# Moving four score steps in front of their slot's projections, and leaving out 18 idle transposes, in a one-core encoder-decoder kernel

## Chip, cores and metric

One Trainium2 chip, one core. The metric is the device time of one execution in microseconds, as the median of several runs. The traces are the hardware profiler's record of one further execution.

## The reference

An encoder layer over a short context, then a decoder layer over a long sequence, all in float32. D = 512, 16 heads of width 32, feed-forward width 2048, two batches, 2048 decoder tokens and 77 context tokens.

```python
x = src                                            # 2 x 77 x 512
x = x + mha(ln(x), ln(x), enc_weights, eb)
memory = x + ff(ln(x))
y = tgt                                            # 2 x 2048 x 512
y = y + mha(ln(y), ln(y), dec_sa_weights, sb)      # causal, with a relative bias
y = y + mha(ln(y), memory, dec_ca_weights, cb)     # cross attention, with a relative bias
y = y + ff(ln(y))
```

`mha` projects to queries, keys and values, takes `softmax(q k^T / sqrt(32) + bias)` per head, multiplies by the values and projects out.

## The kernel before

**Units.** The decoder's self attention is cut into units `(b, m, g, t)`: batch, block of 512 queries, group of four heads, tile of 128 queries; 128 units in all. For each unit the main loop at the end turns the probabilities on TensorE (`turn`, L425), copies them from PSUM (L429 on VectorE, L431 on ScalarE), runs the unit's *slot*, issues scores of a later unit (`scores`, L371), and multiplies by the values (`values`, L442). VectorE adds the bias to the scores and takes their maximum (L380, L387, then L397), and ScalarE takes the exponential (L402). In blocks with m = 0 the four exponentials of a unit are issued with its scores, so they stand in ScalarE's queue ahead of the copies of the turn that follows.

**Slots.** Everything else is hung on slots by hand. `slot(n)` issues three lists in order: `light[n]` (small steps: norms, divisions, loads), `jobs[n]` (projections: `q_job` L215, `k_job` L226, `v_job` L239, `out_job` L251), and `late[n]`. The order is written out: each engine runs its instructions in the order in which they are issued.

**What is in the slots.** The encoder is a chain of stages, put by `encoder()` into the first slots, nearly all into `late`. `score(1)` there (L563) is preceded by 18 transposes of the identity (L560), whose result nobody reads. The first block's cross attention is done inside the self attention of the second batch: `first_cross()` spreads it over slots 65 onwards. For each of four tiles of 128 tokens, t = 0 to 3, the steps are `score` (L783: 16 small products, each 32 rows by 77 columns, into four PSUM banks; then on VectorE for each of four heads L790 where there is a bias (t below 2), L792 and L793), `exp` (L796), `sums` (L801, L802), `normalize` (L807 on GpSimd), `turned` (L813), `times_v` (L824) and `out` (L833). `score` for tile t falls into slot 76 + 3t: slots 76, 79, 82 and 85. The projections in those slots are a key projection (L226), a query projection (L215), a value projection (L239) and a query projection (L215), each eight matmuls of 512 columns.

**Banks.** PSUM has eight banks; bank 7 is kept for the values and seven are given out in rotation, whoever asks:

```python
i = count["bank"] % count["banks"]
count["bank"] += 1
return psum[:, i, :]
```

A projection takes one bank, a score four, a piece of the unit's scores four, each load of a turn one. A step whose bank is still being read by VectorE or ScalarE waits on TensorE, and all that is issued behind it waits too.

## Time and profile before

| | |
|---|---|
| median of 3 runs | 2901.87 us (2894.16 to 2901.92) |
| the profiled execution | 2900.86 us, its span 2898.8 us |
| TensorE (PE) busy | 2861.1 us, 99% of the span |
| VectorE (DVE) busy | 2050.4 us, 71% |
| ScalarE (ACT) busy | 1298.8 us, 45% |
| mean granted TensorE clock | 0.992 |
| slots 76, 79, 82, 85 | score's products start at 1016.9, 1043.5, 1085.1 and 1126.2 us |
| encoder's second score | idle transposes start at 95.2 us, score's products at 97.3 us |

In lines of the trace the first two numbers are the start and the duration in microseconds, then engine, source line, operation, what is written from what, the shapes, and a count; in brackets stands how long the engine idled before it and which instruction ended that. PEld is the loading of weights on TensorE, which runs ahead of the matmuls. A matmul's end is modelled, so small waits hide in it; the distance from one start to the next is the safer measure. A line that covers several instructions merges neighbours of one kind.

### The profile page before, as it was taken

Reading aid. Unit: us, or ns where it says so; the run is one execution under the profiler, and the core shown is the slowest. Engines: PE = TensorE matmul, PEld = TensorE weight load, DVE = VectorE, ACT = ScalarE, POOL = GpSimd, SP = SyncE. Lnnn points to the kernel's source line nnn. Section 1 sums busy time; section 2 is a strip of 40 time slices with the busy share of each in tenths; the row PEclk is TensorE's granted clock in tenths of the full one; section 3 lists DMA queues with packets and bytes.
Section 4 is the critical chain, followed back from the end, with each engine's and each line's share of the span. In section 5 each row is a group of like instructions: output and inputs, shape, how many; then the busy total and the mean of one; then the engine's idle time right before and its main releaser. Section 6 shows DMA issues by size and latency. Waiting matters only on the chain.

```text
span 2898.8 us, 60382 instructions
## 1 busy us (share of the span) xinstructions
PE 2861.1 (99%) x24456; PEld 2025.4 (70%) x24456; DVE 2050.4 (71%) x5566; ACT 1298.8 (45%) x2431; POOL 745.5 (26%) x605
## 2 busy tenths in 40 slices
PE   9899999999999999999999999999999999999999
PEld 5557666666666556666666677777777777777788
DVE  4767688878986668788878895757575757575745
ACT  3344465546665445565556674323232323232321
POOL 0100000000000101100000004464646464646464
PEclk9899999999999999999999999999999999999999
DMA  6413301201112502201201115100002000000000
GB/s 171 116 32 122 107 16 56 63 16 45 34 42 64 138 19 61 76 27 56 63 16 38 42 31 173 37 30 1 29 1 47 1 30 1 30 1 30 1 15 15
DMA packets 118456, 137.34 MB, mean 47 GB/s; under 512 B 18544, under 2 KB 73888, under 8 KB 118050
## 3 DMA queue, kind: packets, MB, share of 16 engines
q1 hardware_dynamic: 118178, 133.49, 15.9%
q8 instruction: 192, 3.15, 0.5%
q14 instruction: 86, 0.70, 0.1%
HBM read 111.59 MB, written 21.86 MB: 46 GB/s over the span
## 4 chain that ended last, share of the span: by engine, by line
PE 93%; DVE 4%; ACT 1%; DMA 1%; issue 1%; SPq 0%; POOL 0%; DVEq 0%; ACTq 0%; POOLq 0%
PE psum L425 17%; PE psum L1198 14%; PE psum L1169 13%; PE psum L371 11%; PE psum L442 9%; PE psum L833 4%; PE psum L768 4%; PE psum L239 4%; PE psum L251 4%; PE psum L215 3%; PE psum L226 3%; PE psum L813 2%; PE psum L783 1%; PE psum L824 1%; ACT pp L402 1%; PE psum L543 1%
## 5 line engine op out<-in xcount | busy, mean ns | idle before, releaser
L402 ACT ACTIVATE pp<-pp,nm 128x128 f32<-128x128 f32 (+15 forms) x512 | 611.6, 1200 | 274.8 <-DVE nm L397 274.6
L380 DVE TENSOR_SCALAR_CACHE_REDUCE pp<-psum 128x512 f32<-128x512 f32 (+3 forms) x1024 | 559.2, 590 | 58.2 <-PE psum L371 56.7
L425 PEld LDWEIGHTS psum<-ident,pp 128*128 128x128 f32 x4352 | 477.2, 143 | 114.6 <-DVE pp L380 51.9
L425 PE MATMUL psum<-ident,pp 128*128 128x128 f32 x4352 | 541.6, 279 | 11.0 <-DVE mx L387 4.4
L431 ACT COPY pts<-psum 128x512 f32<-128x512 f32 (+3 forms) x592 | 297.8, 574 | 477.0 <-PE psum L425 370.9
L1152 POOL TENSOR_TENSOR vv<-pp 128x512 f32<-128x512 f32 x320 | 418.3, 1323 | 153.3 <-PE psum L1169 132.0
L429 DVE COPY pts<-psum 128x512 f32<-128x512 f32 (+2 forms) x544 | 330.0, 659 | 69.0 <-PE psum L425 68.7
L371 PE MATMUL psum<-kT,q 32*128 32x512 f32 (+3 forms) x2560 | 369.0, 577 | 9.8 <-ACT pts L431 4.8
L442 PEld LDWEIGHTS psum<-pts,vv 128*32 128x32 f32 x8704 | 227.3, 110 | 125.4 <-issue 117.3
L442 PE MATMUL psum<-pts,vv 128*32 128x128 f32 x8704 | 280.9, 277 | 0.7 <-ACT pts L431 0.5
L285 POOL TENSOR_TENSOR rstd<-rstd,mhalf 128x1 f32<-128x1 f32 x32 | 18.2, 570 | 881.4 <-DVE rstd L284 881.4
L1184 DVE TENSOR_TENSOR kT<-kT,psum 128x512 f32<-128x512 f32 x256 | 166.0, 680 | 111.5 <-PE psum L1169 102.9
L371 PEld LDWEIGHTS psum<-kT,q 32*128 32x128 f32 x2560 | 128.2, 184 | 148.1 <-issue 86.4
L387 DVE CUSTOM_DVE_ANT_0 pp<-psum,bias 128x256 f32<-128x256 f32 (+1 forms) x512 | 195.9, 411 | 16.4 <-PE psum L371 16.4
L1187 ACT ACTIVATE kT<-kT,vecs 128x256 f32<-128x256 f32 x256 | 115.2, 499 | 176.1 <-DVE kT L1184 176.1
L1198 PE MATMUL psum<-vv 128*128 128x256 f32 x768 | 176.9, 381 | 0.0
L1169 PE MATMUL psum<-oT,vv 128*128 128x256 f32 x736 | 166.5, 380 | 0.0
L1198 PEld LDWEIGHTS psum<-vv 128*128 128x128 f32 x768 | 143.1, 190 | 26.8 <-issue 9.5
L1182 ACT COPY kT<-psum 128x512 f32<-128x512 f32 x124 | 69.6, 588 | 205.3 <-DVE kT L1184 134.9
L1169 PEld LDWEIGHTS psum<-oT,vv 128*128 128x128 f32 x736 | 138.8, 190 | 24.4 <-issue 6.2
L1152 DVE TENSOR_TENSOR vv<-kT 128x512 f32<-128x512 f32 x160 | 136.3, 866 | 12.4 <-PE psum L1198 11.5
L266 POOL TENSOR_TENSOR xr<-xr,row_dec_sa_out_b 128x512 f32<-128x512 f32 x30 | 38.2, 1275 | 370.1 <-DMA xr<-in_x_dram 367.4
(182 smaller groups left out, 3881.1 us busy)
## 6 DMA issues: line engine op xcount, KB each, us to landing
wqk<-in_dec_sa_in_wT_dram SPq DMA_DIRECT2D x64, 256.0 KB, 3.7
bias<-tzg SPq DMA_DIRECT2D x128, 128.0 KB, 3.8
wbig<-in_dec_sa_in_wT_dram SPq DMA_DIRECT2D x8, 1024.0 KB, 5.2
vv<-in_enc_ff_wT_dram SPq DMA_DIRECT2D x8, 1024.0 KB, 5.4
wbig<-in_dec_sa_out_wT_dram SPq DMA_DIRECT2D x8, 1024.0 KB, 5.8
vv<-y SPq DMA_DIRECT2D x32, 256.0 KB, 3.8
out_dram<-vv SPq DMA_DIRECT2D x32, 256.0 KB, 2.0
xt<-in_x_dram SPq DMA_DIRECT2D x30, 256.0 KB, 3.1
```

Of the source, the lines that this page charges most:

```text
L371: nc.tensor.matmul(banks[r][:, : kn * P], q[rows4(r), ts(t, P)], kT[rows4(r), g, k0 * P : (k0 + kn) * P], start=True, stop=True,)
L380: nc.vector.tensor_scalar(p[:, k0 * P : (k0 + far) * P], s[:, : far * P], 1.0, None, ALU.mult, ALU.max, accum_out=st["mx"][:, r, c : c + 1],)
L387: nc.vector.tensor_tensor_reduce(p[:, (i + 1) * P - w : (i + 1) * P], s[:, far * P : kn * P], biases[b, m, g][:, r, 2 * P - w :], 1.0, LOW ...
L402: nc.scalar.activation(p, p, AF.Exp, bias=nm, accum_out=to)
L425: nc.tensor.transpose(pt[:, ts(x, P)], state[n]["p"][r][:, ts(k, P)], ident)
L429: nc.vector.tensor_copy(pts[:, : len(load), :], pt[:, :w])
L431: nc.scalar.copy(pts[:, : len(load), :], pt[:, :w])
L442: nc.tensor.matmul(ot[rows4(r), t, :], vv[:, k, ts(g * HC + r, HD)], got.pop((n, k, r)), start=(k == 0), stop=(k == i),)
L1152: engine.tensor_tensor(dst, quarter(*parts[0], n), quarter(*parts[2], n), SIGN[parts[1]])
L1169: nc.tensor.matmul(mm[:, ts(f, TOK)], a[:, c, ts(f, P)], b[:, c, :], start=(c == 0), stop=(c == 1))
L1184: nc.vector.tensor_tensor(dst, dst, got, SIGN[sign])
L1198: nc.tensor.matmul(mm[:, t, :], lhs[:, c, ts(t, P)], rhs[:, c, :], start=(n == 0 and c == 0), stop=(n == 3 and c == 1),)
```

## The change

The four `score` steps of `first_cross` go from `late` (behind the slot's projection) into `light` (ahead of it). They are entered last into their lists, so they stand behind the slot's other small steps: the division, and `out` of an earlier tile (slots 82 and 85) and the third norm (slot 85). The other steps keep their lists and order. In the encoder the 18 transposes at `score(1)` are gone. No instruction is added; the number of banks taken in each slot is unchanged, their order within the slot isn't.

```diff
             def score(b):
                 banks = [bank() for _ in range(HC)]
-                if b:
-                    for _ in range(18):
-                        nc.tensor.transpose(banks[0][:, :P], ident, ident)
                 for g in range(NC):
...
-            plan, behind = {}, {}
-
-            def at(slot, f, plan=plan):
+            plan = {}
+
+            def at(slot, f):
                 plan.setdefault(slot, []).append(f)
...
                 for k, f in zip((0, 1, 2, 2, 4, 5, 6), fs):
-                    at(11 + 3 * t + k, f, plan if k else behind)
+                    at(11 + 3 * t + k, f)
...
-            return plan, behind
+            return plan
...
-        for fs_of, to in zip(first_cross(), (light, late)):
-            for r, fs in fs_of.items():
-                to[len(units) // 2 + 1 + r] += fs
+        for r, fs in first_cross().items():
+            light[len(units) // 2 + 1 + r] += fs
```

## The prediction

> **What bounds the kernel now.** I read the page first: busy shares and the chain that ended last.

> ```profile
> PE 2861.1 (99%) x24456; PEld 2025.4 (70%) x24456; DVE 2050.4 (71%) x5566; ACT 1298.8 (45%) x2431; POOL 745.5 (26%) x605
> ...
> PE 93%; DVE 4%; ACT 1%; DMA 1%; issue 1%; SPq 0%; POOL 0%; DVEq 0%; ACTq 0%; POOLq 0%
> ```

> TensorE is the bound, so the change is worth what it does to TensorE's stops and to its clock. The table of 4 us windows around the first two scores shows both; the columns are PE, PEld, DVE, ACT, POOL busy (count), granted clock, DMA.

> ```profile
> 1020.00:1024.00 4.00, 1.31 (x15) 0.46 (x3) 3.83 (x9) 0.00 (x0) 0.00 (x0) 0.75 0.00 0
> 1024.00:1028.00 4.00, 3.85 (x9) 2.14 (x10) 1.69 (x12) 2.58 (x10) 0.00 (x0) 0.50 0.00 0
> 1028.00:1032.00 4.00, 4.00 (x23) 1.50 (x22) 1.80 (x5) 1.41 (x3) 0.00 (x0) 0.90 0.00 0
> ...
> 1048.00:1052.00 4.00, 2.64 (x6) 1.28 (x6) 3.86 (x11) 0.00 (x0) 0.00 (x0) 0.66 0.00 0
> 1052.00:1056.00 4.00, 4.00 (x19) 3.59 (x18) 2.88 (x14) 1.27 (x3) 0.00 (x0) 0.50 0.00 0
> ```

> After the scores of slots 76 and 79 PE stops, DVE is full, and the clock is at half. From the means: 0.75 over 4 us is 2 us at half, so it fell at 1022.0; 0.90 in the third row ends it at 1028.8. The second stretch runs likewise from 1049.3 to 1056.1. Then I read the timeline in order of time. Slot 76:

> ```profile
> 1013.33 3.60 PE L226 MATMUL psum<-nT,wqk 128*128 128x512 f32 x8
> ...
> 1016.86 1.13 PE L783 MATMUL psum<-pp 32*128 32x77 f32 x32
> ...
> 1018.01 0.48 DVE L790 TENSOR_TENSOR pp<-psum,pp 128x308 f32<-128x308 f32 x1 [3.16 <-PE psum L783]
> ...
> 1021.37 0.33 PE L425 MATMUL psum<-ident,pp 128*128 128x128 f32 x1 [0.86 <-DVE pp L790]
> ...
> 1024.15 0.48 PE L425 MATMUL psum<-ident,pp 128*128 128x128 f32 x1 [0.89 <-DVE mx L387]
> ...
> 1025.40 5.30 PE L239 MATMUL psum<-wbig,nT 128*128 128x512 f32 x8
> ```

> DVE idles 3.16 us while the key projection runs; then the score's twelve DVE operations (L790, L792, L793 for four heads) hold the banks and keep L387 back, and PE waits. Slot 79:

> ```profile
> 1043.53 0.83 ACT L431 COPY pts<-psum 128x384 f32<-128x384 f32 x2
> ...
> 1044.04 0.86 PEld L783 LDWEIGHTS psum<-pp 32*128 32x128 f32 x26 [0.28 <-ACT pts L431]
> ...
> 1049.77 1.22 PE L371 MATMUL psum<-kT,q 32*128 32x256 f32 x2 [0.72 <-DVE pp L790]
> ```

> Score already waits for ACT there, and PE later waits for DVE. Slot 82:

> ```profile
> 1085.18 0.69 DVE L242 TENSOR_TENSOR vv<-psum,row_sa_bv 128x512 f32<-128x512 f32 x1 [2.74 <-PE psum L239]
> ...
> 1086.30 0.48 DVE L792 TENSOR_REDUCE cmx<-psum 128x4 f32<-128x308 f32 x1 [0.43 <-PE psum L783]
> ...
> 1095.31 0.42 PEld L425 LDWEIGHTS psum<-ident,pp 128*128 128x128 f32 x4 [0.27 <-DVE mx L387]
> ```

> Slot 82 again has a DVE that idles during the projection (2.74 us) and is late afterwards. Last, the encoder's idle turns:

> ```profile
> 95.20 2.19 PE L560 MATMUL psum<-ident 128*128 128x128 f32 x18
> ...
> 98.90 0.83 ACT L431 COPY pts<-psum 128x384 f32<-128x384 f32 x2
> ...
> 99.41 0.71 PE L563 MATMUL psum<-pp 32*77 32x77 f32 x26 [1.73 <-ACT pts L431]
> ```

> **The change part by part.** Score's 16 products (32 instructions) stay as many; PE's work moves by 0.9 us (L783's start 1016.86 to the next weights at 1017.75) and the projection's 3.53 us changes place with it. Score issues no DMA, and POOL and SP are passed by nothing. One SP issue moves with slot 79's projection: the weights that reuse its buffer (L199, 1043.56) go out some 5 us later; slot 83's query projection needs them only at 1097.

> *Which bank.* The turn ahead of slot 76 or 79 fills four of seven banks. Before, the projection took the first free bank, score the next four, so its third head took the turn's first bank, which ACT empties. Now score starts one bank earlier, and its fourth head takes that bank. The projection stands behind that wait in PE's queue.

> *Slot 76.* Score issues at 1013.2, three heads go, the fourth waits for ACT: the copies start at 1013.84 and the first gives its bank 0.51 later (1043.53 to 1044.04 in slot 79), so at 1014.35. From there 0.96 us to the first L790 (1044.04 to 1045.00): 1015.3 instead of 1018.01. The chain to the first L387 took 5.66 us (1018.01 to 1023.67): 1020.97, and PE's fourth turn follows 0.48 later at 1021.45, not 1024.15. PE's own path: projection 1015.2 to 1018.75, scores 0.65, values 1.01, three turns to 1020.6; a wait of 0.9 us is left. L461 and the third L387 put L239's weights at 1022.2 instead of 1025.19. At full clock L239 takes 3.63 us (the next one, 1032.83 to 1036.46), here it took 5.44. So PE is through at 1025.85 instead of 1030.63: **-4.8**. I take the clock to stay, since a key projection and L239 now stand within 4 us of the gap; if it falls all the same, the gain is the 3.0 us of earlier start alone.

> *Slot 79.* Here the same wait is long: score issues at 1039.8, and ACT has four exponentials ahead (1040.70 to 1043.53), so PE stands from 1040.2 to 1044.04, 3.8 us in which the query projection used to run. Score's DVE work starts at 1045.00, as before. The projection runs 1044.9 to 1048.5 beside it; its eviction L217 (0.75 us) now queues behind score's twelve on DVE, and the unit's L380 behind that: 1050.65 + 0.75 = 1051.4, four L380 of 0.48 to 1053.3, L387 0.42, so the next turn's last bank comes at 1053.75. A turn of 0.45 and L813's 1.9 end at 1056.1 against L226's start at 1057.65: -1.5 at best. But 3.8 us of standing should drop the clock. A half-clock stretch of 3.4 to 6.8 us costs PE 1.7 to 3.4; PE's own path from 1048.5 through scores, values, scores, turns and L813 (0.9 + 0.9 + 0.8 + 1.85 + 1.95) ends at 1054.9, so 1056.6 to 1058.3, or 1059.1 if score itself is slowed. Bounds -1.5 and +1.4; I take **-0.5**, by the shorter stretch.

> *Slots 82 and 85.* The copies are done long before (1075.90 to 1079.95, against a score at 1081.5), so no new wait. Slot 82: score's DVE work starts at 1081.5 + 1.22 = 82.7 and takes 3.68 (1086.30 to 1089.98), to 1086.4; L242 0.65, and the first L380 starts at 1087.05 instead of 1089.98, 2.9 earlier, while PE comes to the same L371 at 1086.0. From there PE's work by undisturbed rows is 1.07 + 1.44 + 1.07 + 28 turns x 0.108 = 6.6 us, to 1092.6, the last bank comes at 1092.3; L813 starts at 1092.8 instead of 1095.70: **-2.9**. Slot 85 by the same sum: **-2.8** (DVE 1131.05 to 1128.2). The low end is what PE's rows call idle in 1085.0 to 1097.4 and 1126.2 to 1137.6: 0.4 and 0.24 each.

> Does a gain last? From 1097 to 1126 PE's starts follow each other without a gap, and the later transfers hang on the same steps, so I let it stand.

> *Idle turns.* 18 transposes, 2.19 us of PE, gone; but what follows waits for ACT's copy at 98.90 to 99.35, which nothing on PE moves. Gain zero: PE stands from 95.5 to 99.4 instead. The cost is the clock, which falls anyway at 100.4 and returns at 107.2 (0.55 and 0.60 in the windows from 100 and 104). If it falls 3.4 us sooner, L563 and the work up to 100.4 run slower: 0 to 1.7 us; I take **+0.6**, about L563's 0.7 us doubled.

> *Sum.* -4.8 - 0.5 - 2.9 - 2.8 + 0.6 = -10.4 against the profiled execution's 2900.86 (span 2898.8 and 2.1 around it): 2890.5. That execution lies 1.0 under the median, so 2891 to 2891.5; I say 2891.

> [...] The clock row at 1048 to 1052 fell with PE listed busy 2.64 of 4 us and no idle over 0.72 us; the work was narrow (32-row scores). [...]

> **The rivals.** *The gain is mostly given back* (2896): the clock still falls in slot 76 (-3.0), slot 79 takes +1.4, and slots 82 and 85 save half (-2.8), since DVE is full after 1128 too (3.90 of 4 us) and another release comes late; with +0.6 that is -3.8, or 2897; spread 2894 to 2902. For it: DVE's fullness. Against it: DVE itself starts 2.7 to 2.9 us earlier in three slots.

> *ACT's copy is late in all four slots* (slower): if the exponentials stood ahead of the copies in 82 and 85 as in 79, PE would stand some 3.8 us in each, with a clock stretch each time: 4 x 1.4 + 1.7 = +7.3, 2908; spread 2903 to 2916. It decides once the bank comes about 4 us after score's issue, since then DVE starts no earlier than before. For it: the row at 1044.04. Against it: in slot 76 the bank is 1.1 us away, and in 82 and 85 free.

> That the change does not do what it says I leave at nothing: all four go ahead of a projection.

> **How the numbers follow.** A measurement here can tell about 0.3%, 8.7 us, from no change. Forecast (2884 to 2894): 0.52. Given back: 0.36. Slower: 0.12. The border for faster is 2893.2, which leaves 0.50 faster; the rest of the forecast, the second case and the part of the third under 2910.6 make 0.43 the same; 0.07 slower. The forecast's own range is 2884 to 2894. The range of 2885 to 2901 leaves out the slow case and the tips of the others, under 2 in 10.

> **What would show it.** Right: L783 ahead of L226, L215, L239, L215; slot 76 with a short wait for L431, L239 in about 3.7 us and the clock at 1; slot 79 with a wait of near 3.8 us for L431 and one half-clock stretch over the projection; L380 about 2.9 us sooner after the scores of 82 and 85. Wrong: waits for L431 in 82 or 85, a clock that stays at half beyond 6.8 us in slot 79 or longer in the encoder, or PE gaps of 2 to 3 us that turn up between the slots.

## The result and the profile after

The kernel after takes 2891.58 us (median of 11 runs, 2889.82 to 2894.04) against 2899.01 for the kernel before (11 runs, 2894.16 to 2901.92): a ratio of 0.9974, 95% interval 0.9965 to 0.9983, so 7.4 us less. Repeated in the last set of experiments, it was 2890.91 against 2899.08, ratio 0.9971 (0.996 to 0.9983). The forecast was 2891, in a range of 2885 to 2901; as a difference, -10.4 was forecast and -7.4 measured. The profiled execution took 2889.82 us, the lowest of the 11. In the kernel after the score's lines are three lower: L780 for L783, L787, L789 and L790 for L790, L792 and L793, L810 for L813, L560 for L563.

The page first: TensorE's busy time and the shares of the chain of waits.

```profile
PE 2852.6 (99%) x24438; PEld 2021.1 (70%) x24438; DVE 2048.3 (71%) x5566; ACT 1299.5 (45%) x2431; POOL 746.3 (26%) x605
...
PE 93%; DVE 4%; ACT 1%; DMA 1%; issue 1%; SPq 0%; POOL 0%; DVEq 0%; ACTq 0%; POOLq 0%
```

Nothing there tells where 7 us went; the bound is the same. The windows of 4 us at slots 76 (two rows) and 79 (three) tell it; the columns are those of the tables of before, with the granted clock third from the end.

```profile
1016.00:1020.00 4.00, 3.78 (x51) 2.26 (x50) 3.86 (x15) 0.69 (x1) 0.00 (x0) 1.00 0.25 70
1020.00:1024.00 4.00, 4.00 (x16) 1.45 (x14) 1.68 (x4) 3.94 (x12) 0.00 (x0) 1.00 0.00 0
...
1032.00:1036.00 4.00, 1.44 (x12) 0.98 (x10) 2.08 (x9) 2.78 (x8) 0.00 (x0) 0.97 0.46 124
1036.00:1040.00 4.00, 3.43 (x28) 2.62 (x29) 1.75 (x4) 0.89 (x4) 0.00 (x0) 0.50 0.06 14
1040.00:1044.00 4.00, 4.00 (x7) 1.39 (x5) 3.72 (x9) 0.00 (x0) 0.00 (x0) 0.68 0.00 0
```

In slot 76 PE hardly stops and the clock stays at 1. In slot 79 PE stands (busy 1.44 of 4 us) and the clock is at half from 1035.7 to 1042.6. The timeline of slot 76:

```profile
1011.72 1.11 PE L780 MATMUL psum<-pp 32*128 32x77 f32 x26 [0.58 <-ACT pts L431]
...
1012.66 0.48 DVE L787 TENSOR_TENSOR pp<-psum,pp 128x308 f32<-128x308 f32 x1 [0.56 <-PE psum L780]
...
1018.80 0.33 PE L425 MATMUL psum<-ident,pp 128*128 128x128 f32 x1 [0.21 <-DVE mx L387]
...
1019.63 3.60 PE L239 MATMUL psum<-wbig,nT 128*128 128x512 f32 x8
```

The fourth head waits shortly for ACT's copy, VectorE begins beside the key projection, the waits of 0.86, 1.08 and 0.89 us ahead of the turns are down to one of 0.21, and L239 takes 3.60 instead of 5.30 us. Slot 79:

```profile
1036.57 1.99 PE L780 MATMUL psum<-pp 32*128 32x77 f32 x26 [3.08 <-ACT pts L431]
1038.48 5.70 PE L215 MATMUL psum<-nT,wqk 128*128 128x512 f32 x8
```

Here is the long wait for the copy, and the projection behind it, at half clock for most of its 5.70 us. Slot 82: VectorE's score work, the projection's eviction, the first L380, and the turns' end.

```profile
1075.08 0.48 DVE L789 TENSOR_REDUCE cmx<-psum 128x4 f32<-128x308 f32 x1 [0.42 <-PE psum L780]
...
1078.76 0.68 DVE L242 TENSOR_TENSOR vv<-psum,row_sa_bv 128x512 f32<-128x512 f32 x1
1079.71 0.69 DVE L380 TENSOR_SCALAR_CACHE_REDUCE pp<-psum 128x512 f32<-128x512 f32 x1 [0.27 <-PE psum L371]
...
1085.62 1.91 PE L810 MATMUL psum<-ident,pp 128*77 128x128 f32 x16
```

L242 follows the score's work without an idle time; the 2.74 us of idling are gone.

**Lining up two traces.** Every unit has one L397 on VectorE. Its start in one run minus its start in the kernel before, unit by unit, is a running balance. In the kernel after it stands at -2.74 us ahead of slot 76, and then steps: -4.73 over slot 76, -0.32 over slot 79, -2.40 over slot 82, -2.41 over slot 85, together **-9.86**. It then stays at -12.6 for 370 us, and at 1500 us steps back by +2.1, to -10.44, where it stays. Nothing that the change touches is there. The same work in the timelines, before and then after:

```profile
1509.53 5.14 PE L371 MATMUL psum<-kT,q 32*128 32x256 f32 x18 [0.33 <-DVE pp L380]
1514.60 2.66 PE L425 MATMUL psum<-ident,pp 128*128 128x128 f32 x20
```

```profile
1496.97 6.09 PE L371 MATMUL psum<-kT,q 32*128 32x256 f32 x18 [0.33 <-DVE pp L380]
1503.00 4.22 PE L425 MATMUL psum<-ident,pp 128*128 128x128 f32 x20
```

and the windows there, two of before and then three of after:

```profile
1508.00:1512.00 4.00, 3.67 (x23) 1.95 (x16) 3.68 (x15) 0.00 (x0) 0.00 (x0) 1.00 0.00 0
1512.00:1516.00 4.00, 4.00 (x25) 2.47 (x21) 3.96 (x16) 0.66 (x2) 0.00 (x0) 1.00 0.00 0
```

```profile
1496.00:1500.00 4.00, 3.67 (x22) 2.15 (x18) 3.78 (x15) 0.00 (x0) 0.00 (x0) 0.99 0.00 0
1500.00:1504.00 4.00, 4.00 (x14) 2.18 (x12) 3.97 (x16) 0.00 (x0) 0.00 (x0) 0.50 0.00 0
1504.00:1508.00 4.00, 4.00 (x23) 3.76 (x22) 2.44 (x7) 3.27 (x4) 0.00 (x0) 0.65 0.00 0
```

A half-clock stretch of 6.9 us (0.08 + 4 + 2.8) that the profile of before does not have. The -2.74 ahead of slot 76 is mostly the reverse: the stretch that the profile of before has at 646 us is missing in this one, 2.3 us, and 0.8 us is from the start of the program.

### The profile page after: what moved, and what is told of

It is laid out like the page before. It is cut to its first block, busy times and chain, and to the rows that moved or that the text cites. A ratio compares the mean times of both kernels' runs of the same rounds, so it can differ in the third digit from the quotient of the medians.

```text
span 2888.0 us, 60347 instructions
## 1 busy us (share of the span) xinstructions
PE 2852.6 (99%) x24438; PEld 2021.1 (70%) x24438; DVE 2048.3 (71%) x5566; ACT 1299.5 (45%) x2431; POOL 746.3 (26%) x605
## 4 chain that ended last, share of the span: by engine, by line
PE 93%; DVE 4%; ACT 1%; DMA 1%; issue 1%; SPq 0%; POOL 0%; DVEq 0%; ACTq 0%; POOLq 0%
PE psum L425 17%; PE psum L1194 14%; PE psum L1165 13%; PE psum L371 11%; PE psum L442 8%; PE psum L830 4%; PE psum L765 4%; PE psum L239 4%; PE psum L251 4%; PE psum L215 4%; PE psum L226 3%; PE psum L810 2%; PE psum L780 1%; ACT pp L402 1%; PE psum L821 1%; PE psum L543 1%
## 5 line engine op out<-in xcount | busy, mean ns | idle before, releaser
L380 DVE TENSOR_SCALAR_CACHE_REDUCE pp<-psum 128x512 f32<-128x512 f32 (+3 forms) x1024 | 559.1, 590 | 58.1 <-PE psum L371 56.6
L425 PEld LDWEIGHTS psum<-ident,pp 128*128 128x128 f32 x4352 | 475.0, 142 | 110.2 <-DVE pp L380 51.6
L425 PE MATMUL psum<-ident,pp 128*128 128x128 f32 x4352 | 537.6, 278 | 8.3 <-DVE mx L387 3.7
L431 ACT COPY pts<-psum 128x512 f32<-128x512 f32 (+3 forms) x592 | 297.9, 575 | 473.2 <-PE psum L425 367.0
L371 PE MATMUL psum<-kT,q 32*128 32x512 f32 (+3 forms) x2560 | 362.4, 578 | 5.8 <-ACT pts L431 3.0
L371 PEld LDWEIGHTS psum<-kT,q 32*128 32x128 f32 x2560 | 125.6, 184 | 143.2 <-issue 88.6
L387 DVE CUSTOM_DVE_ANT_0 pp<-psum,bias 128x256 f32<-128x256 f32 (+1 forms) x512 | 195.8, 410 | 16.4 <-PE psum L371 16.4
L1148 DVE TENSOR_TENSOR vv<-kT 128x512 f32<-128x512 f32 x160 | 135.2, 859 | 13.4 <-PE psum L1194 12.4
```

The costliest lines, as they stand in the source:

```text
L371: nc.tensor.matmul(banks[r][:, : kn * P], q[rows4(r), ts(t, P)], kT[rows4(r), g, k0 * P : (k0 + kn) * P], start=True, stop=True,)
L380: nc.vector.tensor_scalar(p[:, k0 * P : (k0 + far) * P], s[:, : far * P], 1.0, None, ALU.mult, ALU.max, accum_out=st["mx"][:, r, c : c + 1],)
L387: nc.vector.tensor_tensor_reduce(p[:, (i + 1) * P - w : (i + 1) * P], s[:, far * P : kn * P], biases[b, m, g][:, r, 2 * P - w :], 1.0, LOW ...
L425: nc.tensor.transpose(pt[:, ts(x, P)], state[n]["p"][r][:, ts(k, P)], ident)
L431: nc.scalar.copy(pts[:, : len(load), :], pt[:, :w])
L1148: engine.tensor_tensor(dst, quarter(*parts[0], n), quarter(*parts[2], n), SIGN[parts[1]])
```

## The experiments

Theory after the result: the four slots give 9.9 us of the 11.0 forecast, and about 2 us go back to half-clock stretches later, which the shift of the work brings about. Rival: some slot gives less in most runs than in this one profile, or the missing turns in the encoder cost it.

**The idle turns alone.**

```diff
-                if b:
-                    for _ in range(18):
-                        nc.tensor.transpose(banks[0][:, :P], ident, ident)
```

> Only the 18 idle turns are left out of the kernel before; the scores stay behind their projections. Theory (the turns filled a wait for ScalarE's copy and only put off the fall of the clock): between 0 and +1.7 us, +0.6 likeliest; in the trace the wait for L431 ahead of L563's 26 weights grows from 1.7 to some 3 us, and the clock falls at about 97 us instead of 100.4. Rival A (the turns were on the path): -2.2 us. Rival B (without them the clock stays low): +3 us or more.

2899.6 against 2899.0 us, ratio 1.0003 (0.9994 to 1.0011). The balance steps by +0.42 between the units around 95 us. Of the trace, PE's wait and the windows:

```profile
99.47 1.19 PE L560 MATMUL psum<-pp 32*77 32x77 f32 x26 [3.16 <-ACT pts L431]
...
96.00:100.00 4.00, 0.84 (x18) 0.69 (x22) 3.69 (x11) 3.88 (x11) 2.49 (x3) 0.67 0.70 126
```

The wait for the copy grew from 1.73 to 3.16 us and the clock fell at 97.4 instead of 100.4; the copy came when it came. The turns were off the path, and by the balance rivals A and B fall; the whole time alone (-1.7 to +3.2 us by its interval) would leave room for B.

**The scores alone.** The turns are put back into the kernel after.

> Only the four scores are moved; the 18 idle turns stay. Theory (all of the gain is in the four slots): the traces of before and after give -4.75, -0.5, -2.4 and -2.4 in slots 76, 79, 82 and 85, so -10 us if nothing is given back. Rival (part is given back between the slots or by the clock elsewhere): -7 us or less, with the missing part to be found in the trace behind slot 85. The turns alone can't explain the difference if they cost under 1 us.

2892.11 against 2899.0, ratio 0.9977 (0.9967 to 0.9986): -6.9. The slots give -4.73, -0.12, -2.40 and -2.41, so -9.66, and at 1502 us the balance steps back by 2.2. The rival: part is given back, and not by the turns.

**One slot at a time.** In the kernel before, the condition that sends a score into the later list is narrowed to some tiles: `t in (0,)`, `t in (1,)`, `t in (2, 3)`.

```diff
-                    at(11 + 3 * t + k, f, plan if k else behind)
+                    at(11 + 3 * t + k, f, plan if k or t in (0,) else behind)
```

> Only tile 0's score (slot 76) is moved; turns stay. Theory (earlier start of the score's VectorE work, 3.0 us, and a clock that no longer falls, 1.8 us): -4.8 us, with the granted clock at 1 through slot 76 and L239 in about 3.7 us. Rival (start alone, clock still falls): -3.0 us. The half-clock stretch of slot 79 stays in either case.

> Only tile 1's score (slot 79) is moved; turns stay. Theory (a stop of some 3.5 us for L431 and a half-clock stretch over the projection, against the VectorE wait and the half-clock stretch that go): -0.5 us, between -1.5 and +1.4. Rival (the stop is what counts): +3 us or more.

> Only the scores of tiles 2 and 3 (slots 82 and 85) are moved; turns stay. Theory (VectorE's idle stretch during the projection takes the score's work): -4.8 us, 2.4 in each slot, and no wait for L431 at the score. Rival (VectorE is full soon after and gives it back): -2 us or less.

| moved | measured against before | ratio, interval | slots, by the balance | later steps of the balance |
|---|---|---|---|---|
| slot 76 | -0.5 us | 0.9998 (0.9989 to 1.0007) | 76: -4.73, 79: +0.58 | +1.6 at 1382, +2.1 at 1508 us |
| slot 79 | +2.1 | 1.0008 (0.9999 to 1.0017) | 79: -0.70 | +1.6 at 1385, +2.1 at 1512 |
| slots 82, 85 | -4.6 | 0.9985 (0.9976 to 0.9994) | -2.40, -2.41 | +1.6 at 1383 |

Each slot does by itself what it does in the whole, within 0.4 us; moving slot 76 alone also shifts the unchanged slot 79 by +0.58. But the medians of the parts, -0.5 + 2.1 - 4.6 and +0.6 for the turns, make -2.4 and not -7.4; on the whole time the expectation for slot 76 was missed by 4 us and that for slot 79 by 2.6, while that for slots 82 and 85 was met within 0.2. The difference stands in the last column: two stretches of narrow work far behind the slots, at about 1383 and 1512 us of the kernel before, which have the full clock there, run at half clock in these kernels. In the run with slot 76 alone, the windows at slot 76 and at the two places:

```profile
1018.00:1022.00 4.00, 3.77 (x51) 2.33 (x44) 3.52 (x15) 1.12 (x4) 0.00 (x0) 1.00 0.24 66
...
1384.00:1388.00 4.00, 4.00 (x62) 3.67 (x54) 1.70 (x5) 2.22 (x5) 1.79 (x2) 0.80 0.16 38
1508.00:1512.00 4.00, 4.00 (x14) 2.08 (x12) 3.96 (x18) 0.00 (x0) 0.00 (x0) 0.56 0.00 0
```

So slot 76 itself behaves as foretold (clock at 1, -4.73), and the whole hides it.

**Shifting the work on purpose.** Idle transposes behind the four slots move all later work without changing it: 22 or 11 in the kernel after, 10 in the kernel before. They write into the bank that is due next, so the rotation of the banks stays.

```diff
+        def stand(k):
+            for _ in range(k):
+                nc.tensor.transpose(psum[:, count["bank"] % count["banks"], :P], ident, ident)
+
+        light[100].append(lambda: stand(10))
```

> The kernel before, with 10 idle transposes (1.07 us) in slot 100. Theory of the grid: the narrow scores at about 1512 us, which keep the full clock in the kernel before, come onto the bad place, so it costs +3.2 us against the kernel before, with a half-clock stretch at about 1513 us in the trace. Rival: +1.1 us and no new stretch.

2902.48 against 2899.08, ratio 1.0011 (1.0002 to 1.002): +3.4. The balance steps by +1.10 at the transposes and by +2.05 at 1511 us, where the clock is now at half:

```profile
1508.00:1512.00 4.00, 3.67 (x17) 2.49 (x16) 3.97 (x18) 0.00 (x0) 0.00 (x0) 0.90 0.00 0
1512.00:1516.00 4.00, 4.00 (x16) 2.18 (x12) 4.00 (x15) 0.38 (x1) 0.00 (x0) 0.50 0.00 0
```

As expected: 1.1 us of delay cost 3.4. The kernel before owes full clock in that place to where the work happens to lie.

> The kernel after, with 22 idle transposes (22 x 0.107 = 2.4 us of TensorE) put into slot 100, behind the four slots. Theory (the half-clock stretches come on a grid of 3.41 us whose place to the work is nearly the same in every run; the change's gain moved the narrow scores near the end of the last block but one onto a bad place of the grid, which takes 2.1 us back at about 1500 us): 2.4 us later the scores lie as in the kernel before, the stretch at 1500 us is gone, and the kernel costs 0 to +0.5 us against the kernel after. Rival (the stretches fall at random, or are none of the gain's doing): +2.4 us.

2894.25 us, 3.3 over the kernel after measured beside it (2890.91, below). The stretch at 1500 us is gone, as expected, but one of two lengths came up at 1378, which I had reckoned safe: the balance steps by +2.40 at the transposes, by +3.24 at 1378, and by nothing at 1500. Half of the expectation held, the total did not.

> The same with 11 idle transposes (1.2 us). Theory of the grid: the narrow work at about 1375 us comes onto the bad place too (1.6 us, as in the runs that moved one slot alone), so it costs between +0.7 and +2.8 us against the kernel after, that is as much as twice 1.2 us or as much as the 22 transposes. Rival: +1.2 us.

2888.14 us, 2.8 **under** the kernel after. In its profile the stretch at 1500 is gone and one of 3.4 us stands at 1374 (+1.6); with the transposes' 1.2 that makes +0.7 behind the four slots, as expected. The profiled execution (2887.57) also lacks the stretches at 520 and 646 us, 3.9 us in all by the balance against the kernel before. They lie ahead of the transposes, which can't have removed them; so it is not shown that the useless work made the kernel faster. Its seven runs lie in two groups, four near 2888 and three from 2891 to 2893, and only the first group's 2887.57 has a profile. On the whole time the expected sign was wrong, and I could not say in advance which narrow place falls.

> The kernel after once more, on the same chip as the three runs with idle transposes: 7.4 us under the kernel before as in its first runs, with a half-clock stretch at about 1500 us and one in slot 79.

2890.91 us, ratio 0.9971 (0.996 to 0.9983); stretches at 1038 (slot 79) and 1502 us, the slots -4.73, -0.18, -2.40 and -2.41.

**What still stands in slot 79.** Two ways against the wait for ACT's copy, both in the kernel after. One only fills it:

```diff
+                        if fill and g == 0 and r == 3:
+                            for _ in range(fill):
+                                nc.tensor.transpose(banks[0][:, 3 * P :], ident, ident)
```

> The kernel after, with 30 idle transposes of the identity in slot 79 between the third head and the fourth of the score, where TensorE stands for L431; they add nothing to the path as long as the wait is over 3.2 us. Theory (the half clock in slot 79 comes of the stop): the clock stays at 1 there, L215 takes 3.6 instead of 5.7 us, and the slot ends 1.3 us sooner, the rest being VectorE's chain. Rival (idle transposes do not hold the clock up): no gain, half clock as before, within 0.5 us of the kernel after.

Slot 79 gives -1.39 instead of -0.32, 1.1 us more, and the projection takes its full-clock time:

```profile
1036.00:1040.00 4.00, 4.00 (x55) 3.83 (x54) 0.54 (x2) 3.32 (x10) 0.00 (x0) 1.00 0.49 137
...
1040.31 3.70 PE L215 MATMUL psum<-nT,wqk 128*128 128x512 f32 x8
```

So the half clock there came of the stop. On the whole, 2892.47 against 2899.37, ratio 0.9976 (0.9967 to 0.9985), it is no better than the kernel after: the stretches at 1377 (+1.6) and 1503 (+2.1) are both there. The 30 transposes stand in the profile as matmuls against the identity (L782, 3.50 us from 1035.84), and the granted clock is 1.00 in all three windows from 1032 to 1044.

The other takes the cause away: three heads go ahead of the projection, the fourth, whose bank ACT still holds, behind it.

```diff
+                    if k == 0 and t < 2:
+                        at(11 + 3 * t, lambda f=f: f(range(3)))
+                        at(11 + 3 * t, lambda f=f: f(range(3, HC)), behind)
+                    else:
+                        at(11 + 3 * t + k, f)
```

> The kernel after, but in slots 76 and 79 only three of the score's four heads go ahead of the projection; the fourth, whose bank ScalarE still holds, goes behind it. Theory (what is left to gain sits in the wait of the fourth head for L431 and the half clock that it brings): the stop of 3.1 us in slot 79 and that of 0.6 us in slot 76 vanish, and the kernel is 3 to 5.5 us under the kernel after, some 12 to 15 us under the kernel before. Rival (VectorE's chain sets the end of slot 79 whatever TensorE does): within 1 us of the kernel after.

2886.12 us against 2899.37, ratio 0.9956 (0.9943 to 0.9968): 13.2 us under the kernel before where the kernel after was 7.4 under it, so some 6 us better. Slot 76 gives -5.04 and slot 79 -5.13; the wait is gone and the clock stays (the score is at L782 in this run):

```profile
1034.21 1.61 PE L782 MATMUL psum<-pp 32*128 32x77 f32 x24
1035.74 3.70 PE L215 MATMUL psum<-nT,wqk 128*128 128x512 f32 x8
1039.38 0.78 PE L782 MATMUL psum<-pp 32*128 32x77 f32 x5
```

It is the best version of this study.

**Does the balance add up to the measured times?** Slots plus the steps at 1383 and 1512 us of each profile and the idle transposes in slot 100, against the medians. What differs ahead of slot 76 is left out, as the moved scores can't cause it:

| kernel | slots | later | sum | measured |
|---|---|---|---|---|
| after | -9.9 | +2.1 | -7.8 | -7.4 |
| scores alone | -9.7 | +2.2 | -7.5 | -6.9 |
| slot 76 | -4.2 | +3.7 | -0.5 | -0.5 |
| slot 79 | -0.8 | +3.7 | +2.9 | +2.1 |
| slots 82, 85 | -4.9 | +1.6 | -3.3 | -4.6 |
| filled wait | -10.9 | +3.7 | -7.2 | -6.9 |
| split heads | -15.0 | +1.6 | -13.4 | -13.2 |
| before, 10 transposes | -0.1 | +3.1 | +3.0 | +3.4 |
| after, 22 transposes | -9.6 | +5.6 | -4.0 | -4.8 |
| after, 11 transposes | -9.9 | +2.8 | -7.1 | -10.9 |
| after once more | -9.7 | +2.2 | -7.5 | -8.2 |

Within 1.3 us but for one, with one profile for each kernel; the slots alone miss by up to 5. The one is 11 transposes, 3.8 us off: its profile lacks the stretches at 520 and 646 us, 3.9 us that the sum leaves out.

## Why the prediction was right, point by point

- **Slot 76, -4.8:** measured -4.73, by the path that was written down: bank released by ACT, first VectorE work 2.6 us sooner (1018.01 less the 2.74 already gained, to 1012.66; 2.7 was forecast), L239 at full clock. The doubt whether the clock would stay was settled by the window at 1.00.
- **Slot 79, -0.5 (bounds -1.5 and +1.4):** -0.32 after, -0.06 to -0.35 in the four other profiles that moved slot 76 too and left the stop as it is, -0.70 with slot 79 alone. The number fits better than the steps behind it. The prediction took the shorter stretch (3.4 us; the profile of before has one of 3.41 us at 520 us and one of 6.83 at 1022), whose own sum is -1.05 (1056.6 against 1057.65); the stretch was the longer one, 6.8 us, whose sum is +0.65. It cost less since it began at 1035.7, while PE still stood (until 1036.57), and the stop was 3.1 us and not 3.8. So the middle value came out partly by luck. The stop, the half clock and the wait for VectorE that it replaces nearly cancel; the filled wait shows that the clock's part is 1.1 us, the split heads that the whole stop was worth 4.8.
- **Slots 82 and 85, -2.9 and -2.8:** -2.40 and -2.41. The mechanism held, the term was 0.5 too large. Score and projection together took 4.7 us on PE (1073.86 to 1078.55) where I had 4.5, L380 started 2.5 and not 2.9 us sooner (1089.98 less the 7.8 already gained, to 1079.71), and the turns then still waited 0.3 us for banks.
- **Idle turns, +0.6:** +0.42 in the balance, +0.6 in the median, though within what a measurement can tell from nothing.
- **"Does a gain last?"** This step failed. I looked as far as 1126 us and let the gain stand; 2.1 us go back at 1500 us, where the clock fell in a window with TensorE listed busy 3.67 of 4 us, a term that the prediction put at nothing. The forecast gain was 3.0 us too large: these 2.1 and 1.1 in the four slots, less 0.2 at the turns. The time came out right all the same, by luck: the sum was taken from 2900.86, 1.9 us over the median of the 11 runs of the kernel before. On the three runs then known the prediction took that execution to be 1.0 under the median.
- **The rivals.** ACT's copy made TensorE wait 3.08 us in slot 79, 0.58 in slot 76 and not at all in slots 82 and 85, as argued. "Mostly given back" named the wrong places: slots 82 and 85 kept 4.8 us, and the loss came where nothing was changed. In size the result (-7.4) lies between it (-3.8) and the forecast (-10.4). At 0.26% it is just short of the 0.3% for faster, so the case with the smaller chance, the same (0.43), came about and not faster (0.50).

## What to carry to other kernels

Work for an idle engine belongs ahead of the long product that it can run beside (-2.4 us in each of slots 82 and 85), but only if its buffers are free there (-0.3 us in slot 79, with a wait of 3.08 us for a bank): look at who holds the last bank of the rotation, and send ahead what has one (-5.1 us there with the heads split). A change of a few microseconds is judged slot by slot, by lining up one recurring instruction in two traces, since the clock's stretches elsewhere can move the total by as much either way (+3.7 us against -4.2 in the slots with slot 76 alone, -3.9 with 11 transposes).

## What the runs showed of the hardware

Half-clock stretches lasted 3.41 us or a multiple of it, except the last one, which runs past the end of the span. The clock records of the profile of before have 3.41 us at 520.2 us and 6.83 us at 646.5, 1022.0 and 1049.3; those of the profile of after have 3.41 us at 520.3 and 6.83 us at 1035.7 and 1499.9. By the means of their windows it was 3.4 us at 1382 us with slot 76 alone and at 1374 with 11 transposes, and 6.9 us at 1378 with 22 transposes and at 1511 in the kernel before with 10. Outside the encoder, the four slots and the end of the program, the stretches of both profiles and of these windows fell at a few places of narrow work (near 520, 646, 1383 and 1512 us of the kernel before), with TensorE listed busy for 3.5 to 4 of 4 us in the windows in which they began, and which of them fell changed with shifts of 1.1 us (10 transposes) and 2.4 us (22 transposes). So 1.1 us of idle transposes cost 3.4 us in the kernel before.

Runs of one kernel differ by up to 8 us, and this goes with the clock: of the 31 runs of the kernel before beside the first four experiments, the eight with a mean granted clock of 0.992 or less took 2900.2 us on average, the seven with 0.994 or more 2896.6. What makes a place of narrow work lose the clock in one run and not in another, and what sets the grid in a run, stays open.
